# Spectral mix: products between the columns of the group before, the spectrum placed by transfers inside SBUF, and mirrored output columns

## The chip, the cores and the metric

The kernel runs on one core of a Trainium2 chip. The time is the device time of one execution in microseconds. Three executions of the kernel before gave 6924.66, 6926.35 and 6928.43 us; the median is 6926.35 us. A separate execution was recorded by the hardware profiler; all durations below come from it.

The engines are named as in the profile: PE multiplies matrices (PEld is its loading of weights), DVE and ACT work element by element and read PE's results from PSUM, POOL works element by element in SBUF and issues some of the transfers, and SP only issues transfers. Each engine, and the queue of transfers on SP, works its instructions in order.

## The reference

Two layers act on x of shape (16, 16, 256, 256) in float32: batch, channel, rows, columns. The changed code computes one term of the first layer.

```python
x = x + _L0_conv_ref(_gn(x), ...)      # layer 0
x = x + _L1_conv_ref(_gn(x), ...)      # layer 1

# in _L0_conv_ref
alpha = jnp.fft.fft2(x, axes=(-2, -1))
A = 1.0 / (omega1[:, None, None, None] - weights_pole1[None])
Bm = 1.0 / (omega2[:, None, None, None] - weights_pole2[None])
S = jnp.einsum('ikpq,oikp,xikq->oxik', weights_residue, A, Bm)
output_residue1 = jnp.einsum('biox,oxik->bkox', alpha, S)
x1 = jnp.fft.ifft2(output_residue1, s=(Ny, Nx), axes=(-2, -1)).real
# x2, from D = alpha . A . Bm and the residues, is added: x1 + x2 / Nx / Ny
```

For every pair of frequencies (o along the rows, x along the columns), the 16 input channels i of `alpha` are multiplied by the 16 x 16 complex matrix S[o, x] to give 16 output channels k. Then the inverse transform is taken, first along the columns and later along the rows.

## The kernel before

The program has four stages that follow one another: `layer0_forward` (normalisation, transform along both axes), `layer0_mix` (the products above and the inverse transform along the columns), `layer0_back` (the inverse transform along the rows, second normalisation) and `layer1` (the convolutions). They hand data on through DRAM: `al` holds the spectrum, `hd` holds what the mix made.

`layer0_mix` goes through the 129 row frequencies that a real input needs in 33 groups g of four (NF = 33; of the last group only one is used). Within a pass of the loop:

- `load_spectrum` (L602 to L611, the transfers are L607) brings the spectrum of one group and of four batch entries (index q, four of them) into a tile `alc`, 128 lanes = four row frequencies x real and imaginary part x 16 channels. There are four such tiles. Each takes four transfers of 32 lanes x 4 KB on SP's queue.
- `expand` (L613 to L619) copies an `alc` tile into `alb`, the operand of the products, with the entries in the order that PE reads. `alb` has a lane for every channel and four blocks j; a mask `m4` keeps in block j only the lanes of its own group of channels and makes the rest zero. `spread` (L629) hands the 16 expansions of a pass out: 6 to ACT (L617) and 10 to DVE (L619), in four portions, one per f.
- `poles` (three DVE operations) and `residues` (L648 to L667) make S for a group: 8 steps of 16 matmuls each (L656) into a PSUM tile `ps`, copied into the tile `s` by ACT and DVE in turn (L667, L665).
- `mix` (L669 to L686) makes the products: four chunks of 64 small matmuls (L679) with weights from `s` and the moving operand `alb[:, i]`, 64 contiguous numbers. ACT copies each chunk from PSUM into `y` (L686). The tiles `ps` and `pg` share two PSUM buffers.
- `turn` (L688 to L702) transposes a quarter f of `y` on PE (L695) into `yt`, with a copy on DVE (L701) and one on ACT (L699).
- `columns` (L704 to L737) makes the inverse transform along the columns for one row frequency f: 16 matmuls (L714) over tables `ix` with 256 columns, even and odd column frequencies apart. ACT copies the odd part (L723), and DVE adds and subtracts (L726, L727), which gives the columns x and x + 128. POOL stores the result with four transfers into `hd` (L734).

PE, ACT, DVE and POOL work in the order in which the program is written (L739 on). In a pass, the first two chunks of products come first, then the other two with the two halves of the last column of the group before between them, and then for each f: a turn, the residues of the next group, its share of the expansion and the column. SP's queue follows the buffers: a load is issued when the expansions that read the tile are done, and it has a whole pass to land. Every transfer also carries one of eight semaphores on SP's queue in turn, and waits until the transfer eight places before it has landed.

Of the kernel before, what the change touches and what calls it, by code (L numbers as in the profile page):

```python
# [10 lines left out]
F32 = mybir.dt.float32  # L11
I32 = mybir.dt.int32
AF = mybir.ActivationFunctionType
ALU = mybir.AluOpType
# [42 lines left out]
def load(nc, pool, src, shape, name):  # L57
    t = pool.tile(shape, F32, tag=name, name=name)
    nc.sync.dma_start(out=t, in_=src)
    return t  # L60
# [505 lines left out]
def layer0_mix(ctx, tc, d, al, hd, tabs):  # L566
# [4 lines left out]
    nb = d["x"].shape[0]  # L571
    cp = ctx.enter_context(tc.tile_pool(name="mc", bufs=1))
    m16 = load(nc, cp, d["m16"], [P, 4], "m16")
    ap = ctx.enter_context(tc.tile_pool(name="ma", bufs=2))
    avd = tabs[1]

    def load_poles(g):
        av = ap.tile([P, 32, 4, 3], F32, tag="av", name="av")
        nc.sync.dma_start(out=av.rearrange("p k f l -> p (k f l)"), in_=avd[g])
        return av  # L580
# [4 lines left out]
    for k in range(0, C // 2, 2):  # L585
        nc.sync.dma_start(out=tt[:, k : k + 2], in_=tabs[0][:, k : k + 2])
    ident = load(nc, cp, d["ident"], [P, P], "ident")
    ix = load(nc, cp, d["ix"], [P, 8, N], "ix")

    alb = cp.tile([P, N, 4, nb], F32, name="alb")
    m4 = load(nc, cp, d["m4"], [P, 4], "m4")

    lp = ctx.enter_context(tc.tile_pool(name="ml", bufs=1))
    gp = ctx.enter_context(tc.tile_pool(name="mg", bufs=1))
# [4 lines left out]

    def load_spectrum(g, q):  # L602

        t = gp.tile([P, 4, 2, P], F32, tag="alc", name="alc", bufs=4)
        src = al[g].rearrange("v (j h c) b x -> h (v j) c (b x)", h=4, c=4)
        for h in range(4):
            nc.sync.dma_start(  # L607
                out=t[32 * h : 32 * h + 32].rearrange("p b e x -> p (b e x)"),
                in_=src[h, :, :, 4 * q * N : 4 * q * N + 4 * N],
            )  # L610
        return t  # L611

    def expand(t, q, j, eng):  # L613

        dst = alb.rearrange("p (x e) j b -> p b e x j", e=2)[:, 4 * q : 4 * q + 4, :, :, j]
        if eng is nc.scalar:
            eng.activation(dst, t, AF.Copy, scale=m4[:, j : j + 1])  # L617
        else:
            eng.tensor_scalar(dst, t, m4[:, j : j + 1], None, ALU.mult)  # L619


    spreads = (
        (((0, 0), (1, 0)), ((0, 1), (0, 2), (0, 3))),
        (((1, 1), (2, 0)), ((1, 2), (1, 3), (2, 1))),
        (((3, 0), (3, 1)), ((2, 2), (2, 3), (3, 2))),
        ((), ((3, 3),)),
    )

    def spread(spectrum, f):  # L629
        for eng, parts in zip((nc.scalar, nc.vector), spreads[f]):  # L630
            for q, j in parts:
                expand(spectrum[q], q, j, eng)

    def poles(av):

# [30 lines left out]
        else:  # L666
            nc.scalar.copy(dst, src)  # L667

    def mix(s, y, between):  # L669


        for x0 in range(0, 64, 16):
            if x0 >= 32:
                next(between, None)
            ps = psg.tile([P, 16, 64], F32, tag="pg", name="pg")
            for x in range(16):
                for q in range(4):
                    i = 4 * (x0 + x) + q
                    nc.tensor.matmul(  # L679
                        ps[32 * q : 32 * q + 32, x],  # L680
                        lhsT=s[:, i].rearrange("p v k -> p (v k)"),
                        rhs=alb[:, i].rearrange("p j b -> p (j b)"),
                        start=True,
                        stop=True,
                    )
            nc.scalar.copy(y[:, :, x0 : x0 + 16], ps.rearrange("p x j -> p j x"))  # L686

    def turn(y, f):  # L688

        yt = hp.tile([P, 8, 8, C], F32, tag="yt", name="yt", bufs=2)  # L690
        for t0 in range(0, 8, 4):
            pt = pst.tile([P, 4, P], F32, tag="pt", name="pt")
            for t in range(4):
                j = 16 * f + 2 * (t0 + t)
                nc.tensor.transpose(pt[:, t], y[:, j : j + 2].rearrange("p q x -> p (q x)"), ident)  # L695
            dst = yt[:, :, t0 : t0 + 4].rearrange("p c t k -> p t c k")
            src = pt.rearrange("p t (c k) -> p t c k", k=C)
            if t0:
                nc.scalar.copy(dst, src)  # L699
            else:  # L700
                nc.vector.tensor_copy(dst, src)  # L701
        return yt  # L702

    def columns(g, f, yt):  # L704

        ph = [psh.tile([P, 2, N], F32, tag="ph", name="ph") for q in range(2)]
        for e in range(2):
            if e:
                yield
            for n, (c, v) in enumerate(((0, 0), (0, 1), (1, 0), (1, 1))):  # L710
                i = 2 * (2 * c + e) + v
                for q in range(2):
                    lanes = slice(64 * q, 64 * q + 64)
                    nc.tensor.matmul(  # L714
                        ph[q][:, e],
                        lhsT=yt[lanes, i].rearrange("p t k -> p (t k)"),
                        rhs=ix[lanes, i],
                        start=n == 0,
                        stop=n == 3,
                    )  # L720
        for q in range(2):
            odd = hp.tile([P, 2, P], F32, tag="odd", name="odd", bufs=2)
            nc.scalar.copy(odd, ph[q][:, 1].rearrange("p (v x) -> p v x", v=2))  # L723
            o = hp.tile([P, 2, 2, P], F32, tag="h", name="h", bufs=5)
            even = ph[q][:, 0].rearrange("p (v x) -> p v x", v=2)
            nc.vector.tensor_tensor(o[:, :, 0], even, odd, ALU.add)  # L726
            nc.vector.tensor_tensor(o[:, :, 1], even, odd, ALU.subtract)  # L727
            o = o.rearrange("p v h x -> p v (h x)")
            fy = 4 * g + f
            for v in range(2):  # L730

                if fy % P or v == 0:
                    part = fy // P if fy % P == 0 else v
                    nc.gpsimd.dma_start(  # L734
                        out=hd[fy % 2, part, fy % P // 2, q:nb:2].rearrange("b k x -> b (k x)"),
                        in_=o[:, v],
                    )  # L737

    E = mybir.EngineType  # L739
    with tc.manual_schedule(engines={E.PE, E.Activation, E.DVE, E.Pool}):  # L740
        spectrum = [load_spectrum(0, q) for q in range(4)]
        lt = poles(av)
        av = load_poles(1)
        s = gp.tile([P, N, 2, C], F32, tag="s", name="s")
        for k0 in range(0, C, 2):
            residues(lt, s, k0)
        for q in range(4):
            spread(spectrum, q)
        for q in range(4):
            spectrum[q] = load_spectrum(1, q)  # L750
        between = iter(())
        for g in range(NF):
            more = g + 1 < NF
            y = gp.tile([P, 64, 64], F32, tag="y", name="y")
            if more:
                lt = poles(av)
            mix(s, y, between)
            if more:
                s = gp.tile([P, N, 2, C], F32, tag="s", name="s")
                residues(lt, s, 0)  # L760
            for f in range(4 if more else 1):
                if more and f == 3:
                    spread(spectrum, f)
                    for k0 in (12, 14):
                        residues(lt, s, k0)
                yt = turn(y, f)
                if more:
                    for k0 in range(2 if f == 0 else 4 * f, 4 * f + 4, 2) if f < 3 else ():
                        residues(lt, s, k0)
                    if f < 3:  # L770
                        spread(spectrum, f)
                    if g + 2 < NF:
                        if f == 0:
                            av = load_poles(g + 2)
                        spectrum[f] = load_spectrum(g + 2, f)
                between = columns(g, f, yt)
                if f < 3:
                    for _ in between:
                        pass


def exponential(nc, pool, y):
# [20 lines left out]
def layer0_back(ctx, tc, d, hd, bd, zn, mr, ed):  # L803
# [34 lines left out]
    def fetch(i):  # L838
# [8 lines left out]
        for e in range(2):  # L847
            nc.sync.dma_start(
                out=h[:, e].rearrange("p k x -> p (k x)"),
                in_=hd[e, :, :, b, k0 : k0 + 4].rearrange("v f k x -> (v f) (k x)"),  # L850
            )
        x = hp.tile([P, 4, 2, N], F32, tag="x", name="x")
        nc.sync.dma_start(
# [568 lines left out]
def fourier_tables():  # L1422
# [5 lines left out]
    def parities(a):  # L1428
# [4 lines left out]
    fy[:, 0, 1, 0] = cos[:P, P]  # L1433
    wx = np.stack([cos, -sin, sin], axis=1)

    wxn = np.stack(
        [
            np.stack([np.concatenate([cos[:P, e::2], -sin[:P, e::2]], 1),
                      np.concatenate([sin[:P, e::2], cos[:P, e::2]], 1)], axis=1)
            for e in (0, 1)  # L1440
        ],
        axis=1,
    )

    ix = np.stack([np.concatenate(a, 1) for a in ((cos[:, :P], sin[:, :P]), (-sin[:, :P], cos[:, :P]))], 1)
    ix = np.tile(ix.reshape(64, 8, N), (2, 1, 1))

    iy = np.stack([cos[:P], -sin[:P]], axis=1) / (N * N)
    iy[0, 0] *= 0.5
# [61 lines left out]
def forward(ctx, tc, d):  # L1511
# [2 lines left out]
    keep = ctx.enter_context(tc.tile_pool(name="keep", bufs=1))  # L1514
    al = dram.tile([NF, 2, 64, nb, N], F32, name="al")
    bd = dram.tile([nb, P, P], F32, name="bd")
    hd = dram.tile([2, 2, 64, nb, C, N], F32, name="hd")
    tabs = (
        dram.tile([P, C // 2, 4, N], F32, name="td"),
        dram.tile([NF, P, 384], F32, name="avd"),  # L1520
# [34 lines left out]
```

## Time and profile before

| | us |
|---|---|
| profiled execution | 6939.37 |
| its span, first to last instruction | 6937.6 |
| first and last matmul of the products (L679) | 1412.6 and 2769.0 |
| PE busy in the span | 6375.2 (92%) |
| DVE busy | 5451.1 (79%) |
| ACT busy | 3703.9 (53%) |
| POOL busy | 3635.8 (52%) |

The page divides the span into 40 slices of 173.4 us and gives each engine's busy share in tenths, PE's granted clock (9 is full) and the busy share of the 16 DMA engines. A group line gives line, engine, operation, tiles (out <- in), shapes and number; behind the first bar the busy time and the mean time of one in ns; behind the second the idle time ahead of it and who ended it. One float32 matmul makes two records. A line of the order of time gives start, length, engine and instructions that follow one another ("x12" is twelve of them). A line of a stretch gives its bounds, the length, each engine's busy time, the granted clock, the share of the DMA engines that is busy, and GB/s.

### The profile page before, as it was taken

How to read it: one execution, taken by the hardware profiler on the slowest of the kernel's cores; microseconds unless marked ns; L12 is line 12 of the kernel's file. 1: busy time of each engine (PE TensorE's matmuls, PEld its weight loads, DVE VectorE, ACT ScalarE, POOL GpSimd, SP SyncE). 2: the span in 40 equal slices, each digit the busy share in tenths (PEclk: the TensorE clock that was granted, in tenths of full speed). 3: DMA queues.
4: the chain of work that ended last, by engine and by line, in shares of the span. 5: the costliest groups of instructions: out<-in, count | busy, mean ns of one | idle time of the engine just before them, and what ended most of it. 6: DMA issues, size and time to landing. Idle time of an engine off the chain costs nothing.

```text
span 6937.6 us, 153382 instructions
## 1 busy us (share of the span) xinstructions
PE 6375.2 (92%) x59944; PEld 3583.2 (52%) x59944; DVE 5451.1 (79%) x10057; ACT 3703.9 (53%) x5732; POOL 3635.8 (52%) x4614
## 2 busy tenths in 40 slices
PE   7899989978888888899789999999999999999996
PEld 5777777766766677677533333333333333333331
DVE  8888987356666666788788888888888888888885
ACT  1223333355655555222376666666666666666671
POOL 2334544523333333666665666666766566665563
PEclk9999999989999999999899999999999999999998
DMA  3444434433333333999877898888988889988886
GB/s 95 124 123 122 122 112 119 113 123 104 111 108 111 110 104 93 318 327 326 281 209 231 272 285 261 264 274 277 286 267 261 272 267 285 287 262 262 272 272 211
DMA packets 715941, 1443.97 MB, mean 208 GB/s; under 512 B 101338, under 2 KB 523542, under 8 KB 672950
## 3 DMA queue, kind: packets, MB, share of 16 engines
q1 hardware_dynamic: 567030, 959.77, 45.0%
q0 software_dynamic: 148192, 474.40, 21.8%
q8 instruction: 478, 7.83, 0.5%
q14 instruction: 241, 1.97, 0.1%
HBM read 877.12 MB, written 556.47 MB: 207 GB/s over the span
## 4 chain that ended last, share of the span: by engine, by line
PE 65%; DVE 20%; DMA 5%; issue 5%; ACT 4%; POOL 1%; SPq 0%; DVEq 0%; ACTq 0%; POOLq 0%
PE c2ps L1201 17%; PE c L1053 14%; PE pd L1121 13%; PE pg L679 4%; PE ph L714 3%; DVE alb L619 3%; ACT wide L1101 3%; PE px L313 2%; PE pu L207 2%; PE py L876 2%; PE pr L1080 2%; PE pv L214 2%; DVE u L224 2%; PE py L877 2%; DVE st L174 1%
## 5 line engine op out<-in xcount | busy, mean ns | idle before, releaser
L1101 ACT ACTIVATE wide<-c,b 32x512 f32<-32x512 f32 x2176 | 1479.6, 680 | 311.6 <-PE c L1053 263.5
L1132 DVE TENSOR_TENSOR top<-pd,t 32x512 f32<-32x512 f32 x2176 | 1504.0, 691 | 52.6
L1053 PE MATMUL c<-z,w 102*128 102x512 f32 x2048 | 999.7, 620 | 110.7 <-ACT wide L1101 89.3
L1113 POOL COPY wide<-wide 32x1031 f32<-32x1031 f32 (+1 forms) x576 | 579.7, 1006 | 881.5 <-ACT wide L1101 854.4
L1129 DVE TENSOR_TENSOR t<-pd,r 64x512 f32<-64x512 f32 x1088 | 744.1, 684 | 345.3 <-PE pd L1121 298.2
L1121 PE MATMUL pd<-wide,dw 128*128 128x512 f32 x2048 | 988.6, 604 | 12.0 <-DVE top L1132 11.0
L734 POOL DMA_DIRECT2D hd<-h x512 | 434.8, 856 | 955.0 <-DVE h L727 937.0
L1053 PEld LDWEIGHTS c<-z,w 102*128 102x128 f32 x2048 | 371.7, 192 | 697.5 <-issue 462.5
L1201 PE MATMUL c2ps<-rows,c 128*32 128x512 f32 x6144 | 721.6, 602 | 5.6 <-DVE odd L1228 5.6
L1121 PEld LDWEIGHTS pd<-wide,dw 128*128 128x128 f32 x2048 | 380.9, 192 | 572.2 <-issue 418.5
L1114 POOL COPY wide<-wide 32x1031 f32<-32x1031 f32 (+1 forms) x576 | 576.0, 1000 | 33.5
L1072 ACT ACTIVATE bot<-c,b 128x512 f32<-128x512 f32 x544 | 344.4, 684 | 462.6 <-issue 381.4
L714 PE MATMUL ph<-ix,yt 64*128 64x256 f32 x4128 | 507.9, 394 | 17.6 <-DVE yt L701 14.7
L313 PE MATMUL px<-wxn,u 128*64 128x256 f32 x4224 | 481.5, 379 | 2.4 <-ACT o L320 2.4
L207 PE MATMUL pu<-fy,eo 128*128 128x128 f32 x2048 | 436.2, 297 | 42.0 <-DVE u L224 35.2
L714 PEld LDWEIGHTS ph<-ix,yt 64*128 64x128 f32 x4128 | 419.6, 192 | 89.9 <-ACT s L667 29.6
L679 PE MATMUL pg<-alb,s 128*32 128x64 f32 x16896 | 311.6, 237 | 154.1 <-issue 71.8
L1201 PEld LDWEIGHTS c2ps<-rows,c 128*32 128x32 f32 x6144 | 174.8, 108 | 513.5 <-issue 404.5
L889 POOL TENSOR_TENSOR x<-x,o 128x512 f32<-128x512 f32 x256 | 324.4, 1267 | 217.3 <-DVE o L888 197.5
L619 DVE TENSOR_SCALAR alb<-alc,m 128x1024 f32<-128x1024 f32 x330 | 424.1, 1415 | 0.0
L214 PE MATMUL pv<-at,eo 128*128 128x128 f32 x2048 | 423.0, 291 | 0.0
L726 DVE TENSOR_TENSOR h<-ph,odd 128x256 f32<-128x256 f32 x258 | 113.4, 440 | 389.4 <-ACT odd L723 389.4
(221 smaller groups left out, 11460.2 us busy)
## 6 DMA issues: line engine op xcount, KB each, us to landing
rows<-cf SPq DMA_DIRECT2D x128, 2176.0 KB
z<-zn SPq DMA_DIRECT2D x768, 257.8 KB
cf<-top POOLq DMA_DIRECT2D x512, 240.0 KB, 6.9
cf<-bot POOLq DMA_DIRECT2D x96, 840.0 KB, 10.8
alc<-al SPq DMA_DIRECT2D x528, 128.0 KB
zn<-zb SPq DMA_DIRECT2D x128, 516.0 KB
o<-zn SPq DMA_DIRECT2D x128, 516.0 KB
z<-in_x SPq DMA_DIRECT2D x64, 1024.0 KB
```

Of the source, the lines that this page charges most:

```text
L313: nc.tensor.matmul(ps[64 * k : 64 * k + 64, :, h], lhsT=u[:, h, part, g0 + j + k].rearrange("p f c -> p (f c)"), rhs=wxn[:, h, part], star ...
L619: eng.tensor_scalar(dst, t, m4[:, j : j + 1], None, ALU.mult)
L679: nc.tensor.matmul(ps[32 * q : 32 * q + 32, x], lhsT=s[:, i].rearrange("p v k -> p (v k)"), rhs=alb[:, i].rearrange("p j b -> p (j b)"), s ...
L714: nc.tensor.matmul(ph[q][:, e], lhsT=yt[lanes, i].rearrange("p t k -> p (t k)"), rhs=ix[lanes, i], start=n == 0, stop=n == 3,)
L1053: nc.tensor.matmul(ps[:, a], lhsT=w, rhs=z[:k, c : c + 2, 0:N], start=True, stop=True)
L1101: nc.scalar.activation(self.feat[64 - 32 * q : 96 - 32 * q, f, self.groups[g], :H], ps[q][32 * f : 32 * f + 32], AF.Mish, bias=b1[0][32 * ...
L1113: nc.gpsimd.tensor_copy(flat[0:32, f, 1:m], flat[64:96, f, 0 : m - 1])
L1114: nc.gpsimd.tensor_copy(flat[96:128, f, 0 : m - 1], flat[32:64, f, 1:m])
L1121: nc.tensor.matmul(ps, lhsT=dwt if self.tail else dw, rhs=self.feat[:, f, cs, :H], start=True, stop=True,)
L1129: nc.vector.tensor_tensor(t[64:128], ps[:64], self.r[:, cs], ALU.mult)
L1132: nc.vector.tensor_tensor(self.top[32 * f : 32 * f + 32, cs, q], ps[lanes], t[lanes], ALU.add)
L1201: nc.tensor.matmul(ps[32 * j : 32 * j + 32], lhsT=w[:, blk], rhs=src[:, 4 * j + blk : 4 * j + blk + 4, x : x + H], start=(i, blk) == (0, 0 ...
```

## The change

The mix is written as two phases for each group. In the first, for each quarter f: the column f of the group before, a chunk of products, two interleaving copies for the next group, the copy of the products to `y`. In the second: all residues of the next group, and all four turns; the turned quarters wait in four `yt` tiles for the next pass.

The expansion with masks is gone. `alb` is laid out with the four blocks outermost and is set to zero once at the start. The spectrum comes in eight portions of two batch entries (tile `alc`, two buffers, four transfers each of 32 lanes x 2 KB). DVE (even portions) and ACT (odd ones) interleave each into a tile `alx` (one buffer). When all eight are there, `place` copies `alx` with 16 transfers inside SBUF into the blocks of `alb`: each takes the 8 lanes 4f + c, 4f + c + 16, ... with 16 KB each. These transfers are issued on SP behind the last loads of the pass. The moving operand of a product is now four runs of 16 numbers.

The transform along the columns is taken at half-sample positions (`wxn` in the forward stage, `ix` here), so that columns x and 255 - x are mirror images: 64 columns are made as a symmetric and an antisymmetric part. Each of the 16 matmuls of a column has 128 moving columns instead of 256. ACT copies the antisymmetric part; DVE makes sum and difference, the latter reversed, and one sum of the halves, POOL the difference. One transfer of twice the size replaces two stores; `hd` keeps even and odd batch entries apart, and the next stage reads it with the same 4 KB rows.

```diff
-    alb = cp.tile([P, N, 4, nb], F32, name="alb")
-    m4 = load(nc, cp, d["m4"], [P, 4], "m4")
+    alb = cp.tile([P, 4, N, nb], F32, name="alb")
+    nc.vector.memset(alb[:, :2], 0.0)
+    nc.gpsimd.memset(alb[:, 2:], 0.0)
...
     def load_spectrum(g, q):
-        t = gp.tile([P, 4, 2, P], F32, tag="alc", name="alc", bufs=4)
+        t = gp.tile([P, 2, N], F32, tag="alc", name="alc", bufs=2)
         src = al[g].rearrange("v (j h c) b x -> h (v j) c (b x)", h=4, c=4)
         for h in range(4):
             nc.sync.dma_start(
-                out=t[32 * h : 32 * h + 32].rearrange("p b e x -> p (b e x)"),
-                in_=src[h, :, :, 4 * q * N : 4 * q * N + 4 * N],
+                out=t[32 * h : 32 * h + 32].rearrange("p b x -> p (b x)"),
+                in_=src[h, :, :, 2 * q * N : 2 * q * N + 2 * N],
             )
         return t
...
+    def interleave(alx, q):
+        dst = alx[:, :, 2 * q : 2 * q + 2]
+        src = spectrum.pop(0).rearrange("p b x -> p x b")
+        if q % 2:
+            nc.scalar.copy(dst, src)
         else:
-            eng.tensor_scalar(dst, t, m4[:, j : j + 1], None, ALU.mult)
+            nc.vector.tensor_copy(dst, src)
+        load_next()
+
+    def place(alx):
+        for f in range(4):
+            for c in range(4):
+                lanes = slice(4 * f + c, P, 16)
+                nc.sync.dma_start(
+                    out=alb[lanes, f].rearrange("p x b -> p (x b)"),
+                    in_=alx[lanes].rearrange("p x b -> p (x b)"),
+                )
...
     def columns(g, f, yt):
-        ph = [psh.tile([P, 2, N], F32, tag="ph", name="ph") for q in range(2)]
+        ph = [psh.tile([P, 2, 4, 64], F32, tag="ph", name="ph") for q in range(2)]
...
+                            ph[q][:, e, blocks],
+                            lhsT=yt[lanes, i].rearrange("p t k -> p (t k)"),
+                            rhs=ix[lanes, i].rearrange("p (b x) -> p b x", b=2),
...
+            anti = hp.tile([P, 2, 2, 64], F32, tag="anti", name="anti", bufs=2)
+            nc.scalar.copy(anti, ph[q][:, :, 2:])
+            w = hp.tile([P, 2, 2, 2, 64], F32, tag="w", name="w", bufs=2)
+            sym = ph[q][:, :, :2]
+            nc.vector.tensor_tensor(w[:, 0], sym, anti, ALU.add)
+            nc.vector.tensor_tensor(w[:, 1, :, :, ::-1], sym, anti, ALU.subtract)
+            o = hp.tile([P, 2, 4, 64], F32, tag="h", name="h", bufs=3)
+            parts = o.rearrange("p v s x -> p s v x")
+            nc.vector.tensor_tensor(parts[:, 0::3], w[:, :, 0], w[:, :, 1], ALU.add)
+            nc.gpsimd.tensor_tensor(parts[:, 2:0:-1], w[:, :, 0], w[:, :, 1], ALU.subtract)
...
+        for g in range(NF):
+            more = g + 1 < NF
+            if more:
+                alx = gp.tile([P, N, nb], F32, tag="alx", name="alx")
+            y = gp.tile([P, 64, 64], F32, tag="y", name="y")
+            for f in range(4):
+                if g:
+                    columns(g - 1, f, yts[f])
+                ps = mix(s, y, 16 * f)
+                if more:
+                    for q in (2 * f, 2 * f + 1):
+                        interleave(alx, q)
+                nc.scalar.copy(y[:, :, 16 * f : 16 * f + 16], ps.rearrange("p x j -> p j x"))
+                if more and f == 1:
+                    lt = poles(av)
+                    if g + 2 < NF:
+                        av = load_poles(g + 2)
+            yts = []
+            if more:
+                place(alx)
+                s = gp.tile([P, N, 2, C], F32, tag="s", name="s")
+                for f in range(4):
+                    for k0 in (4 * f, 4 * f + 2):
+                        residues(lt, s, k0)
+                    yts.append(turn(y, f))
+            else:
+                columns(g, 0, turn(y, 0))
```

## The prediction, made before the changed kernel was run

> **What bounds the kernel now.** I read the page first, to find the stage that the change touches: the mix runs from the first matmul of L679 at 1412.6 us to 2769.0 us, slices 8 to 15.
>
> ```profile
> span 6937.6 us, 153382 instructions
> PE   7899989978888888899789999999999999999996
> PEclk9999999989999999999899999999999999999998
> DMA  3444434433333333999877898888988889988886
> ```
>
> In those slices PE is busy 8 to 9 tenths and the transfers 3 tenths. The span's other 5.5 ms are the same code in both kernels, so the working concerns the 33 passes of the mix loop. From the first L679 matmul of pass 0 to that of pass 32 go 1342.3 us, 41.95 us a pass. Next, the groups of instructions of 1395 to 2795 us:
>
> ```profile
> L714 PE MATMUL ph<-ix,yt 64*128 64x256 f32 x4128 | 507.9, 394 | 17.6 <-DVE yt L701 14.7 <-ACT yt L699 0.7 <-issue 0.6
> L619 DVE TENSOR_SCALAR alb<-alc,m 128x1024 f32<-128x1024 f32 x330 | 424.1, 1415 | 0.0
> L617 ACT ACTIVATE alb<-alc,m 128x1024 f32<-128x1024 f32 x198 | 387.5, 2059 | 1.3 <-DMA alc<-al 1.3
> L679 PE MATMUL pg<-alb,s 128*32 128x64 f32 x16896 | 311.6, 237 | 154.1 <-issue 71.8 <-DVE s L665 68.7 <-DMA alc<-al 13.2
> L665 DVE COPY s<-ps 128x1024 f32<-128x1024 f32 x131 | 159.8, 1220 | 40.6 <-PE ps L656 40.0
> L686 ACT COPY y<-pg 128x1024 f32<-128x1024 f32 x132 | 133.7, 1013 | 422.4 <-PE pg L679 422.4
> ```
>
> Then the order of time in one pass, for the pace of each piece:
>
> ```profile
> 1992.05 13.64 SPq L607 DMA_DIRECT2D alc<-al  x12
> ...
> 1993.09 1.96 PE L656 MATMUL ps<-tt,lt 64*32 64x256 f32 x64
> ...
> 1995.17 3.73 PE L714 MATMUL ph<-ix,yt 64*128 64x256 f32 x32
> ...
> 1996.30 3.86 DVE L619 TENSOR_SCALAR alb<-alc,m 128x1024 f32<-128x1024 f32 x3
> ...
> 2000.71 1.09 PE L695 MATMUL pt<-ident,y 128*128 128x128 f32 x8
> ...
> 2017.70 1.99 PE L679 MATMUL pg<-alb,s 128*32 128x64 f32 x128
> ```
>
> PE works in a written order: 4 columns of 3.73, 8 residues of 0.98, 4 turns of 1.09, 4 chunks of products at about 2.0 plus 4 us in which the first two chunks stall on "issue": about 39 us, and 2 us of waiting for DVE's last copy of s. DVE (10 expansions, 13 us) is the co-bound. SP is idle most of the pass: 16 loads at 0.69 us. Last, how fast transfers go, from busy stretches of the third stage (the last two columns are the DMA share and GB/s):
>
> ```profile
> 1424.00:2755.00 1331.00, 1166.15 (x29311) 935.75 (x29314) 845.71 (x1177) 779.29 (x828) 431.17 (x506) 0.95 0.35 106
> 5066.00:5070.00 4.00, 4.00 (x31) 1.12 (x33) 3.63 (x7) 3.85 (x7) 3.50 (x4) 1.00 0.87 204
> 6767.00:6774.00 7.00, 7.00 (x31) 2.48 (x30) 6.73 (x11) 3.23 (x6) 5.34 (x11) 1.00 1.03 411
> ```
>
> At 6767 full-height rows move with all 16 engines busy at 411 GB/s, 25.7 GB/s an engine. At 5066 only z loads of 32 lanes each (L1033) are under way: 0.87 of 16 engines move 204 GB/s, 14.7 GB/s an engine. Few lanes at a time nearly halve an engine.
>
> **The change, part by part.** All times are per pass.
>
> *Columns on half the moving operand.* 32 matmul records of 256 columns take 3.73 us; each row half of the array runs one per 216 ns and the halves overlap. With 128 columns the nearest row is L207 (128 columns, full-size weights): one record per 111 ns. Two halves side by side: 16 x 0.112 = 1.8 us, a gain of 1.9 a column; 0 at the other end. PE's list is then 4 x (1.85 + 2.1) + 7.9 + 4.4 = 28 us, and the stalls on "issue" vanish between the columns. The weight loads could forbid this: their records in L714 take 187 ns, but those of the two halves start 36 ns apart and run together. [...] The row decides.
>
> *Expansion removed.* 10 x 1.29 us of DVE and 6 x 1.96 of ACT go; 4 interleaving copies of 512 elements come on each. DVE: 0.69 (the 512-element yt copy), down to 0.4 if reading SBUF helps, up to 0.72 (half of L619's 1.415). ACT: 0.6 (the yt copy's 0.586), up to 1.03 (half of L617, if the narrow writes cost it the same). DVE's third and POOL's new operation in columns (0.33 behind another; 0.75 by L265's 753 ns) lie in idle time of 48 us, as do POOL's issues: 8 instead of 16, of twice the rows, at 0.6 to 0.86. The stores write the same bytes.
>
> *Loads.* 16 of 128 KB become 32 of 64 KB on SP, in two buffers instead of four. They keep their 32 rows, so 0.69 us each: 2.76 a buffer. The first of a batch lands 1.98 us after its issue ends; half the bytes lower that to 1.7, stores in the way raise it to 2.6: I take 2.0. A buffer is asked for again only when its copy is done, so a pass holds three round trips where four buffers stood ready. Behind a late load stand, on ACT, the copy to y that frees a product buffer and the next column's two copies; on DVE, the next column's adds, for which PE's second next column waits.
>
> *Placing.* 16 transfers of 8 lanes x 16 KB, between the last load of the pass and the first product of the next. They wait on SP behind 8 loads, and L679 and the next interleaving copies (same tile alx) wait for all 16. Matching shapes issue in about 0.37 us (L579: 0.32), so data decides. The alc loads have 8 outer rows in DRAM, and in 97% of their time no more than 8 of their packets are under way: 8 engines. From the first issue to the first data go 1.65 us. At 25.8 GB/s an engine (159 ns per 4 KB, alc's median) 2.1 MB take 10.2 us; at 14.7 they take 17.8; nothing in the trace goes from SBUF to SBUF, and if both ends pay, 36. I take 18.5 (the 590 ns that a z packet of 8,248 bytes takes in those bursts give 18.75), since 8 lanes at a time are nearer to 32 than to 128. [...]
>
> *The sum*, from the moment that a placing has landed (0): first copy done 0.7. Product chunk 0 to 4.2 (PE has idled, and the trace's clock records show half speed for 3.4 to 6.8 us at nearly every turn of a pass), its copy to y 5.4, column 1 to 6.2, two ACT copies 7.1, six DVE adds 8.85, second DVE copy 9.5. Load 12.3, landed 14.4, copy 15.1. Load 17.9; the last copy waits behind the adds of column 3, which follow ACT's y copy: 21.9. Two loads for the next pass but one, ahead of the placing on SP: 27.5. Placing 1.65 + 18.5 + 0.3: 48.0. PE's residues and turns run from 24.4 to 38.3, the next column to 40.1: 8 us of PE idle.
>
> 48.0 - 41.95 = 6.05, times 32 passes = +194. Start: four round trips (1389.2 + 4 x 5.6 + 2.8 + 2.8 = 1417) and a placing (20.5) put the first product at 1438 instead of 1412.6: +25. The two memsets (8192 elements; L1011 sets 4128 in 3.55 us, so 7) end before. Last pass: no change, 23 us in both. Together +219: 7158 on the profiled execution's 6939.4, which lies 13 us above the median; 7145 against 6926.
>
> **The rivals.**
> *Placing at full engine speed* (10.2 us): it lands at 39.7, while PE's own list ends with column 0 at 40. A pass takes 40: -1.95 x 32 = -62, start +17: 6881, the other sign. For it: alc on 8 engines runs at 25.8 GB/s. Against: alc covers 32 lanes, this 8. It decides below 0.75 us a transfer (12.0 in all).
> *Both ends pay*: 36 us, a pass of 65.5: 23.5 x 32 = 754, start +42: 7722. For: source and destination are the same lanes. Against: loads and stores overlap today without a visible sum.
> *Columns do not shorten*: 1.9 us on column 1 alone, as column 0 lies beside the placing: +60, 7205.
> *Landing in 2.6 us and ACT at 1.03*: +1 us a pass in the main case, and +1 to +2 in the first rival, which then ends at about 6925.
>
> **How the numbers follow.** Main case with its variants 0.66 (own range 7080 to 7300: placing 16.5 to 23), first rival 0.25, both ends 0.09. In the first rival four of five outcomes are faster by over 0.2% (what a measurement of this kernel can tell from none, 14 us): faster 0.21, same 0.04, slower 0.75. The range of 8 in 10 takes the first rival and the main case and leaves out the third: 6855 to 7300.
>
> **What would show it.** Placing transfers lasting over 1.1 us each, SP's and DVE's copies waiting for "alb" or "alx", PE idle 6 to 10 us before the first L684 matmul of a pass, clock at half there, DVE and ACT under 50% in the stage (64% and 59% now), a pass of 46 to 50 us; L719 at about 57 ns a record. I am wrong if 16 placings land within 12 us, or if loads are asked for earlier than their buffers suggest.

## The result and the profile after

The changed kernel takes 7303.08 us (median of 4 runs, 7298.45 to 7314.37), the kernel before 6925.51 beside it (4 runs, 6913.88 to 6928.43): 1.0551 times as long, with a 95% interval of 1.0533 to 1.0569. The profiled execution took 7302.35 us with a span of 7300.6; against the span of before that is 363 us more.

The page of the changed kernel, its span and rows of the 40 slices:

```profile
span 7300.6 us, 155453 instructions
PE   7999989666666666689978999999999999999996
ACT  1223333222323232322237666666666666666661
PEclk9999999878888788799989999999999999999998
DMA  3444434444444444489987789988888998888886
```

The mix now runs from 1435.0 to 3130.7 us, slices 7 to 16 and the start of 17, counted from 0 as in the prediction (a slice is 182.5 us here). TensorE has gone from 8 or 9 tenths to 6 there, ScalarE to 2 or 3, the granted clock to 7 or 8, and the transfers only from 3 to 4: no engine is busy for more than 6 tenths of slices 7 to 16. The groups of the mix stretch (1435 to 3140 us; busy time, mean ns of one, then the idle time in front of them and what ended it):

```profile
L684 PE MATMUL pg<-alb,s 128*32 128x64 f32 x16896 | 325.6, 243 | 439.2 <-DMA alb<-alx 410.1 <-issue 28.8
L719 PE MATMUL ph<-ix,yt 64*128 64x128 f32 x4128 | 305.4, 288 | 30.2 <-DVE w L732 29.0 <-ACT yt L704 0.7 <-ACT alx L628 0.5
L665 PE MATMUL ps<-tt,lt 64*32 64x256 f32 x8192 | 301.8, 427 | 181.8 <-ACT y L774 180.6 <-issue 1.1
L630 DVE COPY alx<-alc 128x512 f32<-128x512 f32 x128 | 97.0, 758 | 337.3 <-DMA alb<-alx 307.1 <-DMA alc<-al 30.1
L628 ACT COPY alx<-alc 128x512 f32<-128x512 f32 x128 | 94.7, 740 | 763.4 <-DMA alc<-al 386.2 <-DMA alb<-alx 376.6 <-issue 0.6
```

TensorE waits 410 us for the placing, 12.4 us in each of 33 passes, and another 181 us for the copies to y, which stand on ScalarE behind interleaving copies that wait for loads (386 us). One pass in the order of time shows both:

```profile
2199.91 18.47 SPq L638 DMA_DIRECT2D alb<-alx  x16
2209.57 2.06 PE L719 MATMUL ph<-ix,yt 64*128 64x128 f32 x32
2214.27 0.72 POOL L740 DMA_DIRECT2D hd<-h  x1 [0.30 <-DVE w L732]
2216.05 0.72 POOL L740 DMA_DIRECT2D hd<-h  x1 [0.30 <-POOL h L736]
2223.89 3.64 PE L684 MATMUL pg<-alb,s 128*32 128x64 f32 x128 [12.26 <-DMA alb<-alx]
2223.97 14.24 SPq L608 DMA_DIRECT2D alc<-al  x16
2233.12 0.96 DVE L630 COPY alx<-alc 128x512 f32<-128x512 f32 x1
2241.95 0.74 ACT L628 COPY alx<-alc 128x512 f32<-128x512 f32 x1 [6.50 <-DMA alc<-al]
2242.59 1.01 ACT L774 COPY y<-pg 128x1024 f32<-128x1024 f32 x1
2246.23 0.95 DVE L630 COPY alx<-alc 128x512 f32<-128x512 f32 x1
2252.98 3.71 SPq L638 DMA_DIRECT2D alb<-alx  x4
```

The placing is issued from 2199.91 on, and the first product comes at 2223.89, 24 us later. Column 0 is done at 2211.6 and TensorE then stands still. In the other part of the pass, 29 us from the first product to the next placing, ScalarE waits 6.5 us for a load, the copy to y follows it, VectorE's last interleaving copy comes at 2246.23, and eight loads later SP reaches the next placing.

Over all passes the period is 52.47 us against 41.95. Its two parts are means over passes 1 to 31 (52.57 together; pass 0, without columns, is shorter): 23.78 from the first issue of a placing to the first product (1.26 to the first data, 21.78 of data, 0.74 after them), and 28.78 from there to the next placing. 32 x 10.52 = 337 us of the 363; 22 more are the later start (1435.0 against 1412.6), and 4 lie in the last pass and behind it. The rest of the program takes the same time in both.

### The profile page after: what moved, and what is told of

It is laid out like the page before. It is cut to its first block, busy times and chain, and to the rows that moved or that the text cites. A ratio compares the mean times of both kernels' runs of the same rounds, so it can differ in the third digit from the quotient of the medians.

```text
span 7300.6 us, 155453 instructions
## 1 busy us (share of the span) xinstructions
PE 6241.8 (85%) x59944; PEld 3467.6 (47%) x59944; DVE 5283.1 (72%) x10118; ACT 3408.3 (47%) x5666; POOL 3627.6 (50%) x4619
## 5 line engine op out<-in xcount | busy, mean ns | idle before, releaser
L1141 DVE TENSOR_TENSOR top<-pd,t 32x512 f32<-32x512 f32 x2176 | 1504.3, 691 | 52.5
L736 POOL TENSOR_TENSOR h<-w 128x256 f32<-128x256 f32 x258 | 233.4, 905 | 1252.1 <-DVE w L732 1249.3
L684 PEld LDWEIGHTS pg<-alb,s 128*32 128x32 f32 x16896 | 297.9, 126 | 461.2 <-issue 449.2
L665 PE MATMUL ps<-tt,lt 64*32 64x256 f32 x8448 | 314.1, 430 | 216.5 <-ACT y L774 180.6
L628 ACT COPY alx<-alc 128x512 f32<-128x512 f32 x132 | 97.7, 740 | 795.9 <-DMA alc<-al 418.6
L731 DVE TENSOR_TENSOR w<-ph,anti 128x256 f32<-128x256 f32 x258 | 108.3, 420 | 398.7 <-ACT anti L728 398.7
```

The source lines that it names most:

```text
L684: nc.tensor.matmul(ps[32 * q : 32 * q + 32, x], lhsT=s[:, i].rearrange("p v k -> p (v k)"), rhs=alb[:, :, N // 2 * (i % 2) + i // 2], star ...
L1141: nc.vector.tensor_tensor(self.top[32 * f : 32 * f + 32, cs, q], ps[lanes], t[lanes], ALU.add)
```

## The experiments

Kernels of one group ran on one chip beside the kernel before: e1 to e4 (before: 6913.85 us), e5 to e8 (6908.99), e9 to e11 (6915.89), e12 (6915.21). Where no interval is given, there is one execution, and the reading rests on its trace. "Placing" is the time from the first issue of a placing to the first product, "stretch" that from the first product to the next placing, both as means over passes 1 to 31.

**e1, other lanes for the placing**

```diff
-                lanes = slice(4 * f + c, P, 16)
+                lanes = slice(4 * f + c, 4 * f + c + 96, 12)
```

> The 16 placing transfers keep their number, their 8 lanes of 16 KB and their place in the order, but take the lanes 4f+c+12i (i = 0 to 7) instead of 4f+c+16j. What lands in alb is therefore not what the products need: the output is not the reference's, the work is the same. In the changed kernel a 16 KB packet of the placing takes 1.24 us (median), 8 packets are under way, and from the first issue of a placing to the first product go 23.8 us of a pass of 52.8. Theory A, the lanes meet in few ways into SBUF: with other lanes the packets fall towards 0.62 us (their shortest today is 0.611), the placing to 12 to 14 us, the pass to 41 to 43 us, the time to 6930 to 7000 us. Theory B, a transfer engine moves half as much from SBUF to SBUF as from DRAM, whatever the lanes: packets stay at 1.2 us, the pass at 52 to 53, the time at 7290 to 7320. Theory C, the issues on SP (1.2 us each today) set the pace: as B in time, but with packets of 0.62 us and gaps between them.

7037.51 us. The 16 KB packets fell from 1.24 us (median) to 0.82, the data from 21.78 us to 13.61, the placing from 23.78 to 15.62; the stretch stayed (28.76 against 28.78), and the pass is 44.28. Busy time by engine, granted clock, DMA share and GB/s in the middle of the first placing, where no stores run, first in the changed kernel, then in e1:

```profile
1415.00:1432.00 17.00, 2.10 (x64) 0.90 (x64) 2.19 (x2) 1.04 (x1) 0.00 (x0) 0.65 0.50 110
```

```profile
1418.00:1429.00 11.00, 2.42 (x80) 1.11 (x64) 2.45 (x2) 1.07 (x2) 0.00 (x0) 0.81 0.48 155
```

Both keep half of the 16 engines busy, with 8 rows each; the lanes alone make it 110 or 155 GB/s. In that placing the data take 19.99 us and 13.41. (In the later passes no store runs beside the shorter placing of e1, so a part of the step from 21.78 to 13.61 comes from that.) Theory A holds as far as the lanes decide, and B and C fall; that the lanes meet in few ways into SBUF was the author's explanation, and no run shows it. All of A's figures were missed: the packets stop at 0.82 us, not at 0.62, so something else limits them from there on, and placing, pass and time lie above its ranges.

**e2, the columns alone**, added to the kernel before

```diff
-    ix = load(nc, cp, d["ix"], [P, 8, N], "ix")
+    ix = load(nc, cp, d["ix"], [P, 8, P], "ix")
...
-        ph = [psh.tile([P, 2, N], F32, tag="ph", name="ph") for q in range(2)]
+        ph = [psh.tile([P, 2, 4, 64], F32, tag="ph", name="ph") for q in range(2)]
```

> The kernel before with the mirrored columns alone (narrow moving operand, three additions on VectorE and one on GpSimd, one store per half), its expansion with ten products on VectorE and six on ScalarE kept. In the changed kernel a column takes 2.05 us on TensorE instead of 3.73, so TensorE's list of 39 us a pass loses 6.7. Theory A, the columns are worth what TensorE saves: pass 35.5 to 38 us instead of 41.95, time 6930 - 32 x (4 to 6.5) = 6720 to 6800. Theory B, VectorE becomes the bound (it loses nothing of its 13 us of expansions and gains a third addition at 0.42 us for each of 8 halves, 3.4 us): pass 40 to 42, time 6870 to 6930.

6974.66 us, 1.0088 times before (1.0064 to 1.0112): slower, and outside both expectations. The pass is 43.24 us instead of 41.95. What TensorE waits for in 1410 to 2800 us (total, times, longest):

```profile
PE ph L716 <- DVE yt L701: 146.2, 62, 3.2
PE pg L679 <- DVE s L665: 140.8, 32, 5.4
PEld ph L716 <- ACT alb L617: 115.0, 32, 3.6
```

It is near theory B, and more: VectorE keeps its expansions and gets a third addition, TensorE waits for its copies of yt and s (68.7 us for s in the kernel before) and for ScalarE's expansions, and the 6.7 us saved on TensorE come back as waiting. VectorE is busy for 910 of the 1300 us from 1450 to 2750, so it is late rather than full.

**e3, the lanes in another order**, so that a block's lanes are evenly spaced over all 128

```diff
-        for f in range(4):
-            for c in range(4):
-                lanes = slice(4 * f + c, P, 16)
+        for f in range(4):
+            lanes = slice(f, P, 4)
...
-                lhsT=lt[lanes, kk, g, 1 - v : 3 - v].rearrange("p l f c -> p (l f c)"),
+                lhsT=lt[lanes, kk, g, v].rearrange("p c l f -> p (c l f)"),
...
-        src = al[g].rearrange("v (j h c) b x -> h (v j) c (b x)", h=4, c=4)
+        src = al[g].rearrange("(j r) v b x -> j (r v) (b x)", j=4)
```

> The changed kernel with another order of the 128 lanes: f in the two low bits, so that a block's lanes are f, f+4, f+8 ... and 4 transfers of 32 lanes replace 16 of 8. The spectrum in DRAM is stored in the order that makes each load 32 evenly spaced rows; the poles' table gets a fourth multiplication on VectorE to pay for the order, and the columns' output tile two buffers instead of three to pay for its room. Theory A (few ways into SBUF): all 16 engines, packets of 0.61 to 0.65 us, data of a placing in 5 to 6 us, first issue to first product 7 to 9 us; with the 29.0 us from the first product to the next placing that gives 36 to 38, less than TensorE's residues and turns allow (they end 13.9 us after the fourth chunk's copy, near 40), so a pass of 39 to 41 and 6870 to 6930 us. Theory B (half rate from SBUF to SBUF, 13 GB/s an engine): packets of 1.2 us on 16 engines, data 10 us, placing 12 to 13, pass 41 to 43, time 6930 to 7000.

7005.93 us, 1.0136 times before (1.0112 to 1.0161). In the middle of the first placing:

```profile
1408.00:1413.00 5.00, 2.20 (x64) 1.00 (x64) 2.34 (x2) 1.04 (x1) 0.00 (x0) 1.00 1.00 311
```

All 16 engines move 311 GB/s; the data of a placing take 7.5 us, between the 5 to 6 of theory A and the 10 of B, in packets of 0.83 us. TensorE no longer waits for the placing. Yet the pass is 43.6 us, above every expectation: the stretch grew to 31.5, where ScalarE waits for late loads in front of the copies to y, and TensorE for those:

```profile
ACT alx L628 <- DMA alc<-al: 279.2, 48, 8.1
PE ps L665 <- ACT y L774: 86.5, 28, 6.2
```

(Totals of 1900 to 2600 us.) With the placing cured, late loads are what the chain waits for. The longer stretch has other possible sources too: this kernel also gives VectorE a fourth multiplication of the poles and the columns' output two buffers in place of three, and no run parts their shares.

**e4, four load buffers in the changed kernel**

```diff
-        t = gp.tile([P, 2, N], F32, tag="alc", name="alc", bufs=2)
+        t = gp.tile([P, 2, N], F32, tag="alc", name="alc", bufs=4)
```

> The changed kernel with four alc buffers instead of two (the columns' w gets one buffer instead of two and their output two instead of three, for the room). The placing is as in the changed kernel, 23.8 us. Theory A, the 29.0 us from the first product of a pass to the next placing are load round trips (a copy, four issues of 0.69 us, a landing of 2 us): with two more buffers they shrink to 22 to 25, the pass to 46 to 49, the time to 7090 to 7190. Theory B, they are set by VectorE's and ScalarE's order (copies behind the additions of the columns and the copies of the products) and by eight loads ahead of the placing on SP: 28 to 30, pass 52 to 54, time 7280 to 7340.

7214.56 us. The placing is the same (24.01), the stretch 25.47 instead of 28.78, the pass 49.48: a little short of theory A. Two buffers instead of four cost 3.3 us a pass.

**e5, the order alone**

```diff
+                nc.scalar.copy(y[:, :, 16 * f : 16 * f + 16], ps.rearrange("p x j -> p j x"))
                 if more:
                     for q in (2 * f, 2 * f + 1):
                         interleave(alx, q)
-                nc.scalar.copy(y[:, :, 16 * f : 16 * f + 16], ps.rearrange("p x j -> p j x"))
...
                 place(alx)
+                load_next()
+                load_next()
```

> The changed kernel with its order alone altered: on ScalarE the copy of a product buffer to y goes ahead of the interleaving copies instead of behind them, and on SP the two loads that open the next pass go behind the placing instead of ahead of it. The placing keeps its 16 transfers of 8 lanes. Theory A: of the 29.0 us from the first product of a pass to the next placing, 5.6 (eight issues of 0.69) are queueing on SP and 2 to 3 the copies held by late loads: 20 to 23 us remain, a pass of 44 to 47, 7040 to 7130 us. Theory B: the loads' round trips alone need the 29 us (four rounds of a copy, four issues and a landing, 5.5 to 6.3 each, 22 to 25, then the placing at once): 24 to 25, a pass of 48, 7150 to 7170.

7187.22 us, a pass of 49.14: stretch 25.66, placing 23.56. Theory B, and a little more: the round trips need 25 us even when nothing stands in front of the placing (it starts 0.12 us after the last copy, in place of 4.3).

**e6 and e7, the swapped lanes with that order, and then with two copies ahead of the pass**

```diff
                     yts.append(turn(y, f))
+                    if f == 2 and g + 2 < NF:
+                        nxt = ahead()
```

> The kernel with swapped lanes (4 placing transfers of 32 lanes) with the same two changes of order. Its pass is 43.6 us now, with TensorE waiting 5 to 7 us at a time for the copy to y, which waits behind an interleaving copy whose load is late. Theory A: those waits go, and the pass falls to TensorE's own list with its half-clock stretches, 31 to 35 us: 7006 - 32 x (8.6 to 12.6) = 6600 to 6730. Theory B: the loads' round trips stay in front of the placing (22 to 25 us, and 8 for the placing and its landing): 32 to 34 us if the placing starts at once, 36 to 38 if copies wait behind the columns' additions; 6700 to 6830.

> As the run before it, and the first two interleaving copies of a pass move into the stretch of residues and turns, where the placing has just landed, so that the loads of the third and fourth piece start 6 us or more sooner. Theory A (loads in front of the placing decide): 2 to 6 us a pass less than the run before it, 30 to 32 us, 6550 to 6640. Theory B (TensorE's list decides already): no difference beyond 1 us a pass.

e6: 6832.30 us, 0.9889 times before (0.9874 to 0.9903), a pass of 38.59, just past the slow edge of theory B. e7: 6780.18 us, 0.9814 (0.9792 to 0.9836), a pass of 36.77: 1.8 us less, short of the 2 to 6 of its theory A and more than B allowed; its level lies far above the 30 to 32 of A. Loads in front of the placing still hold both kernels up. In e7 ScalarE still waits for them (1900 to 2600 us):

```profile
ACT alx L628 <- DMA alc<-al: 214.4, 63, 7.2
```

**e8, e7 with the wide columns of the kernel before** (256 columns of moving operand, two additions a half)

```diff
-    ix = load(nc, cp, d["ix"], [P, 8, P], "ix")
+    ix = load(nc, cp, d["ix"], [P, 8, N], "ix")
...
-        ph = [psh.tile([P, 2, 4, 64], F32, tag="ph", name="ph") for q in range(2)]
+        ph = [psh.tile([P, 2, N], F32, tag="ph", name="ph") for q in range(2)]
```

> As the run before it, with the columns of the kernel before (256 columns of moving operand, two additions per half, two stores): what the mirrored columns alone are worth when nothing else waits. A wide column takes 3.73 us on TensorE instead of 2.05, four of them 6.7 us a pass. Theory A: the whole 6.7 us come back, 32 x 6.7 = 215 us more than the run before it. Theory B: VectorE (8 x 0.42 + 8 x 0.1 us a pass less) or the loads decide, and less than half of it comes back, under 100 us.

6798.41 us, 0.9837 (0.9822 to 0.9852), beside 6780.18 for e7: 18 us, with intervals that overlap. Theory B. The passes are 37.18 and 36.77. Halving TensorE's work in the columns is worth next to nothing in e7 too.

**e9, four buffers, four copies ahead, column 0 among the residues**

```diff
-        interleave(alx, 0)
-        interleave(alx, 1)
+        for q in range(4):
+            interleave(alx, q)
...
+                    if f == 2:
+                        columns(g, 0, yts[0])
```

> The kernel of e7 with four load buffers instead of two, the first four interleaving copies ahead of the pass instead of two, column 0 moved from ahead of the first products into the stretch of residues and turns (so that three tiles yt do for four), and all loads ahead of the placing again. Theory A, in e7 the late loads still decide (ScalarE waits 214 us for them in 19 passes, in front of the columns' copies): a pass falls from 36.8 to 31 to 33.5 us, 6600 to 6680 us. Theory B, the chain copy of the odd half, additions, next column's psum buffer decides, or the placing's own 13 us beside 14 us of residues and turns: 35 to 37 us, 6720 to 6790.

6849.48 us, 0.9906 (0.9888 to 0.9924), a pass of 38.75: slower than e7, against both theories. All copies come first, so all loads are issued in one go:

```profile
2007.38 22.27 SPq L608 DMA_DIRECT2D alc<-al  x32
```

32 issues at 0.7 us fill most of the stretch of 25.3, and the pieces that the pass still needs are in that queue. So more buffers did not help here. One more thing differs from e7: the two loads that e7 issued behind the placing stand ahead of it again. e9 alone does not part this from the rest; e12 goes on with SP's issues.

**e10, the columns' difference on VectorE**

```diff
-            nc.gpsimd.tensor_tensor(parts[:, 2:0:-1], w[:, :, 0], w[:, :, 1], ALU.subtract)
+            nc.vector.tensor_tensor(parts[:, 2:0:-1], w[:, :, 0], w[:, :, 1], ALU.subtract)
```

> The changed kernel with the columns' difference moved from GpSimd to VectorE, so that GpSimd computes nothing in this stage. In the changed kernel VectorE's interleaving copy takes 0.44 us where GpSimd is not in that subtraction and 0.96 us where it is. Theory A, the two engines keep each other out: every copy at 0.43 to 0.46 us; the last copy of a pass is 0.5 sooner, the eight additions at 0.42 more are behind loads, so the pass stays within 1 us of 52.5, 7270 to 7340 us. Theory B, the place in the pass (transfers in flight, half clock) makes the copies slow: they stay at 0.9 to 1.0.

7337.10 us, a pass of 53.55. The copy's group in 1435 to 3160 us, to be read beside the L630 line of the changed kernel above:

```profile
L630 DVE COPY alx<-alc 128x512 f32<-128x512 f32 x127 | 56.9, 448 | 244.5 <-DMA alb<-alx 177.2 <-DMA alc<-al 37.0 <-issue 30.2
```

448 ns on the mean instead of 758, nearly all at 0.43 to 0.44 us: theory A, as far as the copy goes.

**e11, column 0 behind the first products**

```diff
-                if g:
+                if g and f:
                     columns(g - 1, f, yts[f])
                 ps = mix(s, y, 16 * f)
+                if g and f == 0:
+                    columns(g - 1, f, yts[f])
```

> The changed kernel with column 0 behind the first chunk of products instead of ahead of it: two stores of 128 KB each leave the stretch in which the placing runs, the placing itself is the same. In the changed kernel the placing's data take 20.0 us in pass 0 without stores beside it, 21.1 in pass 1 with 262 KB, 21.8 in the others with 524 KB. Theory A, stores and placing share the way: 20.5 to 21.2 us of data, placing 22.5 to 23.2 instead of 23.8. Theory B, the stores cost the placing nothing (the later passes differ by something else): 21.6 to 22.0. The pass as a whole: 52 to 55 us, 7280 to 7390, as the column's 2 us and its additions now stand in the other stretch.

7430.82 us. No store runs beside the placing any more (513 KB in the changed kernel), its data take 20.05 us instead of 21.78, and the placing 22.37 instead of 23.78: theory A, a little below its range. (A store has 262 KB, not the 128 of the expectation's first sentence.) The pass of 56.4 and the time lie above what was expected, because the column's copies now hold back the first interleaving copy on ScalarE (it ends about 7.5 us after the first product, not 0.65), and the stretch grows by 5.5 us.

**e12, e9 with loads of twice the size**

```diff
-        t = gp.tile([P, 2, N], F32, tag="alc", name="alc", bufs=4)
+        t = gp.tile([P, 4, N], F32, tag="alc", name="alc", bufs=2)
...
-        dst = alx[:, :, 2 * q : 2 * q + 2]
+        dst = alx[:, :, 4 * q : 4 * q + 4]
...
+                if more and 0 < f < 3:
+                    interleave(alx, f + 1)
```

> The kernel of e9 with 16 loads of 128 KB a pass instead of 32 of 64 KB (four pieces of four batch columns, two buffers of 16 KB rows' quarter), four interleaving copies instead of eight, the first two ahead of the pass. In e9 SP issues 32 loads at 0.69 us in one stretch of 22 us, and copies, additions and products behind them wait. Theory A, the issues on SP are what remains in front of the placing: 11 us of them go, TensorE's list of 28 us with its half-clock stretches and the placing beside residues and turns decide: 32.5 to 35 us a pass instead of 38.75 (36.8 in e7), 6640 to 6730 us. Theory B, landings and the chain of copies decide, not the issues: 36 to 38.5 us, 6760 to 6840.

6727.30 us, 0.9726 times before (0.9713 to 0.9739), faster than both kernels; a pass of 35.23, at the slow edge of theory A. Rows of its page:

```profile
span 6732.1 us, 153709 instructions
PE   7889989978888888999799999999999999999996
DVE  8888997446666666888688888888888888888884
PEclk9999999989999999999899999999999999999998
```

and the end of one pass:

```profile
2025.88 2.36 SPq L608 DMA_DIRECT2D alc<-al  x4
2028.68 2.50 PE L684 MATMUL pg<-alb,s 128*32 128x64 f32 x128
2031.25 4.51 SPq L637 DMA_DIRECT2D alb<-alx  x4
```

The loads are in the queue before the last products are done, the placing starts as these end (0.22 us later on the mean), and its landing is 6.1 us earlier than the next products can start. TensorE is at 8 tenths again, the granted clock at 9 but for one slice: the change pays once transfers are out of its way. With half the issues there are also half the interleaving copies, and no run parts the two; nor does one show what the two-phase order is worth without the other parts of the change.

## Why the prediction was wrong

The sign and the chain of waits were right; two terms of the sum were too small, and the reason given for the larger of them was wrong: +363 us on the profiled pair where the sum gave +219, so that 7303 lies just above the range's 7300. The start was right within 3 us (1435.0 against 1438). Nearly all of the difference is in the pass: 52.5 us where the chain gave 48.0, and 32 x 4.5 = 143. Point by point:

**Columns, 1.85 us.** 32 records take 2.05 us, 64 ns each; the two halves of the array do overlap, as their starts had shown (in the column at 2209.57 they start in pairs, 7 ns apart, one pair per 105 ns). That the gain would lie beside the placing, and only column 1 count, was right in kind.

**Interleaving copies, 0.69 and 0.6 us.** 0.44 or 0.96 on VectorE (e10 shows what parts them), 0.74 on ScalarE. The sum of these is small.

**Issue of a placing transfer, 0.37 us.** The median is 1.2 us, but data decide, as assumed: in e1 the same 16 issues end sooner because the data do, which is what theory C denied.

**Placing, 1.65 + 18.5 + 0.3.** This is the first term that was mis-sized: 1.26 + 21.78 + 0.74 = 23.8 instead of 20.45, 3.3 of the 4.5 us. (The loads of the kernel before do not show the 1.65 either: after a pause, 1.43 us pass from an issue to the first 4 KB packet, the median.) The step says "I take 18.5 (the 590 ns that a z packet of 8,248 bytes takes in those bursts give 18.75), since 8 lanes at a time are nearer to 32 than to 128". Twice 590 ns was near: a 16 KB packet takes 1.24 us, and a placing with no store beside it (pass 0, and all passes of e11) 20.0 us. That only 8 of the 16 engines would work was right too (a share of 0.50). But the reason behind the row, "Few lanes at a time nearly halve an engine", does not hold: with other lanes a packet takes not 1.24 us but 0.82 where a transfer has 8 lanes (e1) and 0.83 where it has 32 (e3). Which lanes they are makes the difference, not how few, so the nearness of 18.5 was luck. The larger part, 1.7 us, is missing altogether: column 0 was put beside the placing, and its stores of 513 KB were given no price there. The data take 20.0 us in pass 0 without stores, 21.1 in pass 1 with half of them, 21.8 later; e11 moves column 0 away, and the stores with it, and gets 20.05.

**Landing of a load, "I take 2.0".** The second mis-sized term. The ScalarE copy of the third chunk starts 3.0 us (median) after its load's last issue, above the upper bound of 2.6. The 64 KB loads land among the columns' stores, 1.6 MB in each stretch, and the trace points at these: the fourth piece of a pass, with no store beside it, is copied 1.95 us after its last issue, the fifth, with some 260 KB of stores, 2.95. No run takes the stores away from the loads, so this cause is not shown; the poles' transfer, which SP issues right behind the sixth piece (the one of that ScalarE copy), may have a share, as in pass 0, without stores, that piece took 2.8 and the third to fifth 1.9 to 2.0. The copy to y, column 3 and the additions follow, and the last VectorE copy ends at 22.9 us where the sum had 21.9; the issues behind it add 0.3. That is the 28.8 us in place of 27.5. The structure of this part of the chain, round trips with ScalarE's copy to y and VectorE's additions behind them, was right: four buffers (e4) or another order (e5) each take about 3 us off, neither more.

**The rivals.** Placing at full engine speed needed 0.75 us a transfer; it took 1.36 (21.8 / 16). With other lanes it comes nearer, but not to its sign: e1 moves the same bytes in the same number of transfers in 13.6 us, still above 12.0, and lands at 1.0179 times before (7037.51 / 6913.85, one execution). "Both ends pay" gave 36 us and fell. "Columns do not shorten" fell as a time of the column, but its message was truer than the main case: e8 and e2 show that shorter columns are worth 18 us in one kernel and cost 61 in another.

**What was to show it.** Transfers over 1.1 us each, copies and products waiting for alb and alx, the first chunk at nearly half pace (3.64 us where the next ones take 1.99), VectorE and ScalarE under 50% (680 and 495 of 1670 us) all came. TensorE's idle time of 12.4 us a pass and the pass of 52.5 were above the 6 to 10 and 46 to 50 given.

## What to carry to other kernels

Before a transfer between lanes goes onto the critical path, count the engines that its rows keep busy (half of the 16 with 8 rows, all with e3's 32) and see how the lanes lie. Here reordering lanes so that each block takes every fourth lane, with 4 transfers of 32 lanes in place of 16 of 8, made the placing's data 2.8 times as fast (19.99 to 7.08 us in pass 0, where no stores run), and the kernel could then be made 2.7% faster than before, with the next waits met in turn: late loads, then the queue of SP's issues. Price a transfer with the stores that run beside it: here 21.8 us of data with 513 KB of stores, 20.0 with none. And work saved on one engine counts only up to the wait that follows it: TensorE's 6.7 us a pass in the columns were worth 0.4 us in e7 and less than nothing in e2.

## What the runs showed of the hardware

**Lanes and engines.** The same 2.1 MB within SBUF moved at 110 GB/s with 8 engines and lanes 4f+c+16j, at 155 with 8 engines and lanes 4f+c+12i, at 311 with 16 engines and lanes f+4i. The packets took 1.24, 0.82 and 0.83 us. So the first form is held by its lanes, and the other two by something that gives an engine 20 GB/s (16,384 bytes in 0.82 us), against 25.8 for the loads from DRAM (4 KB in 159 ns in the kernel before). Why the first lanes are slower, and what limits the other two, no run shows.

**Half of the engines.** The placing's transfers with 8 rows kept a share of 0.50 (changed kernel) and 0.48 (e1) of the engines busy, though SP had issued the next ones already; those with 32 rows kept 1.00 (e3). In the changed kernel's first placing 8 of its packets were under way for 80% of the time, and hardly ever more. Which eight engines they are, and why the others get none, the traces do not tell.

**VectorE and GpSimd.** A copy of 512 elements a lane within SBUF takes 0.44 us alone, 0.43 beside a store's issue on GpSimd, and 0.96 where a subtraction on GpSimd is beside it too (medians of 41, 4 and 76 of the 132 copies); with that subtraction on VectorE nearly all take 0.43 to 0.44. The prediction had taken one figure in between. By what the subtraction holds the copy up, no run shows.
